# Edge sums of a graph kernel: from TensorE products in step 0 to VectorE and ScalarE in step 1

## The chip, the core and the metric

The kernel runs on one core of a Trainium2 chip. Its engines are TensorE (PE in the profile, with PEld for its weight loads), VectorE (DVE), ScalarE (ACT), GpSimd (POOL) and SyncE (SP); each takes its instructions from its own queue. The metric is the device time of one execution in microseconds (us), less is better.

## What is computed

Four graph layers over 4096 nodes with 256 features each, all with the same 0/1 adjacency of 4096 x 4096, each layer with a residual and a layer norm. Layer 1 is the long one: two steps, and in each a row-normalised neighbour product (`R @ Xf`) and a top-p attention (`A @ Xa`).

```python
# layer 0
agg = adj @ x / jnp.maximum(deg, 1.0)
relu(concat([x, agg]) @ W + b)
# layer 1, for n in range(2)
A = _top_p_attention(Xa, W1, W2, W3)
Xf = R @ Xf
Xa = A @ Xa
Z = Z + Xf @ U1[n].T + Xa @ U2[n].T
# layer 2, called with edge_features = adj
neighbor_node_features = adj @ node_features
neighbor_edge_features = jnp.einsum('ij,ji->i', adj, edge_features)[:, None]
support = concat((node_features, neighbor_node_features, neighbor_edge_features))
return support @ weight + bias
# layer 3
out = A_norm @ x
relu(out @ W + b)
```

The change concerns `neighbor_edge_features`: for each node i the sum over j of `adj[i, j] * adj[j, i]`. Both factors are 0 or 1, so it is the number of edges that exist in both directions. The kernel holds it in `nef`, one column for each tile of 128 nodes, and layer 2 alone reads it.

## The kernel before

The 4096 nodes are 32 tiles (NT) of 128 rows. Layer 0 reads the adjacency as float32, turns it into bytes (u8) on the way, and stores the bytes in device memory as `adj8_d`, one block for each tile. Layers 2 and 3 stream the adjacency again.

Layer 1 is built by `run_step(n, es)`, once for each step n. Its loop goes over i from -2 to 31. In one turn three tiles are at work: tile i is weighted with its attention and multiplied out (`st`), tile i + 1 has its threshold found (`cd`), and the logits of tile i + 2 are made (`nxt`). `pieces` writes this turn out in 8 chunks (NLC) of 512 nodes. A chunk holds the logits of `nxt` (`logits_chunk`, copied from PSUM to `e` by ACT at L381), the attention product of `st`, a chunk of a neighbour product (`neighbours`) and small operations given in `ops`. In step 0 attention is sparse: 16 rows gathered by POOL (`gather`, L638) and multiplied by diagonal matrices (L729). In step 1 it is dense: transposes (L712), a copy to `at` by ACT (L715), and matmuls (L737). DVE looks for the largest logits (MAX8, L399, L494), takes single values out (MATCH_REPLACE8, L624) and masks what falls below the threshold (L629). ACT makes the exponentials, in step 1 of a whole row of 4096 in one instruction (L422). Rows whose threshold needs more search are put off and done by a second pass (`put_off`, names ending in `_l`).

`neighbours(n, i, g, acc_r, pn, xf)` is the neighbour product of tile i, chunk g: SP loads 8 blocks of bytes for two chunks (`adj8`, three buffers), ACT widens them to `adjq` (L649), PE multiplies four blocks of 128 x 512 into `acc_r` (L652). Where `pn` is given, which is in step 0 only, it also makes the edge sums: POOL loads blocks of the other orientation as bytes (`adjn8`, L658), ACT widens them (L661), and PE multiplies the same four `adjq` blocks by them into `pn` (L664). After all 32 blocks the diagonal of `pn` is what is wanted; DVE multiplies by the identity and sums (L678) in `r_end`. `pn` lies in the PSUM buffer tagged `nef`. Because of that, step 0's `acc_r` has the one buffer `acc`, and `r_acc` lets tiles alternate between `acc` and `nef` only after `nef_done`.

Neighbour products need no attention, so they run ahead where PE is free: four tiles before the first attention tile of step 0, the first five of step 1 at the end of step 0, six more at the start of step 1 (`FIRST`), and one in a turn after that.

After a tile, `after` mixes both results (`mix`, L790 and L792), and in step 1 takes two layer norms, in each of which DVE makes the variance, POOL the power -1/2 (`rstd`, L192) and DVE the rest (L816, L197). POOL also writes the list of rows that are put off (L572). SP loads what `fetch` asks for (L773) and stores results (L761, L680).

The program is not executed in the order of the text: a scheduler places the instructions of each engine into one fixed order when the program is built, by priority and by its own idea of when operands are there. Waits between engines are semaphores. A buffer of a pool (`bufs=2`) is given out again when its last reader is done, and the instruction that writes it next waits for that in its engine's queue.

Of the kernel before, what the change touches and what calls it, by code (L numbers as in the profile page):

```python
# [21 lines left out]
P = 128  # L22
# [23 lines left out]


@with_exitstack
def gnn_stack(ctx, tc, x, adjt, adjn, w0, b0, w1, w2t, w3t, u1t, u2t, ln_g, ln_b, w2, b2, w3, b3, out):

# [267 lines left out]

    with tc.tile_pool(name="l1", bufs=1, reuse_waits="tile") as l1:

        cur = {"late": False, "n": 0, "nef_done": False}


        FIRST = [[range(k * NT // 16, (k + 1) * NT // 16) for k in range(2)]]
# [61 lines left out]
        def small(tag, w=1, dt=F32, bufs=2):  # L388
            if cur["late"]:
                return cur["lw"].tile([P, w], dt, tag=tag, name=f"{tag}_l", bufs=2 if w == 1 else 1)  # L390
            return work.tile([P, w], dt, tag=tag, name=tag, bufs=bufs)
# [248 lines left out]

        GP = LC // P

        def neighbours(n, i, g, acc_r, pn, xf):

            if g % 2 == 0:
                cur["a8"] = cur["w"].tile([P, 2 * GP, P], U8, tag="adj8", name="adj8", bufs=3)
                nc.sync.dma_start(cur["a8"], adj8_d[i][:, g * GP : (g + 2) * GP, :])
            a = cur["w"].tile([P, GP, P], F32R, tag="adjq", name="adjq", bufs=2)
            nc.scalar.copy(a, cur["a8"][:, g % 2 * GP : (g % 2 + 1) * GP, :])  # L649
            for j in range(GP):  # L650
                jt = g * GP + j
                nc.tensor.matmul(acc_r, a[:, j, :], xf[:, jt, :], start=(jt == 0), stop=False)  # L652
            if g + 1 == NLC:
                nc.tensor.matmul(acc_r, ident_r, xf[:, i, :], start=False, stop=True)
            if pn is not None:
                if g % (NLC // 2) == 0:
                    cur["b8"] = cur["w"].tile([P, NT // 2, P], U8, tag="adjn8", name="adjn8", bufs=2)
                    nc.gpsimd.dma_start(cur["b8"], adjn[i, :, g * GP : g * GP + NT // 2, :])  # L658
                b = cur["w"].tile([P, GP, P], F32R, tag="adjn", name="adjn", bufs=2)
                k = g % (NLC // 2) * GP  # L660
                nc.scalar.copy(b, cur["b8"][:, k : k + GP, :])  # L661
                for j in range(GP):
                    jt = g * GP + j
                    nc.tensor.matmul(pn[:, :P], a[:, j, :], b[:, j, :], start=(jt == 0),  # L664
                                     stop=(jt == NT - 1))

        def r_acc(i):

            return ps_acc.tile([P, 512], F32, tag=("acc", "nef")[i % 2 if cur["nef_done"] else 0], name="acc_r", bufs=1)

        def r_end(i, acc_r, pn):
            xf_new = work.tile([P, D], F32, tag="xf_new", name="xf_new", bufs=1)
            nc.scalar.activation(xf_new, acc_r[:, :D], AF.Copy, scale=rs[:, i : i + 1])
            nc.vector.scalar_tensor_tensor(xf_new, acc_r[:, D:], rs[:, i : i + 1], xf_new, op0=ALU.mult, op1=ALU.add)
            if pn is not None:

                junk = spare_row.bitcast(F32)[:, :P]
                nc.vector.scalar_tensor_tensor(junk, pn[:, :P], 1.0, ident, op0=ALU.mult, op1=ALU.mult,  # L678
                                               accum_out=nef[:, i : i + 1])
            nc.sync.dma_start(rows(xf_d, i), xf_new)  # L680

        def r_product(n, i, xf):

            acc_r, pn = r_acc(i), None
            if n == 0:
                pn = ps_acc.tile([P, 512], F32, tag="nef", name="nef_ps", bufs=1)
            for g in range(NLC):
                neighbours(n, i, g, acc_r, pn, xf)
            r_end(i, acc_r, pn)

        def pieces(n, st, nxt, ops, rs_now=()):


            G = GP
            few = st is not None and sparse(st)
            if st is not None:
                e = st["e"]
                acc_a = half("acc")
                if "xf" not in st:
                    fetch(n, st)  # L700
            with_r = st is not None and len(rs_now) > 0
            if with_r:
                i, = rs_now
                acc_r, pn = r_acc(i), None
                if n == 0:
                    pn = ps_acc.tile([P, 512], F32, tag="nef", name="nef_ps", bufs=1)
            ats = {}

            def turn(g):
                ps = ps_tr.tile([P, 4, P], F32, tag="tr", name="at_ps")  # L710
                for j in range(G):
                    nc.tensor.transpose(ps[:, j, :], e[:, (g * G + j) * P : (g * G + j + 1) * P], ident)  # L712
                at = cur["w"].tile([P, G, P], F32, tag="at", name="at", bufs=2)
                ats[g] = at
                nc.scalar.copy(at[:, :G, :], ps[:, :G, :])  # L715

            if st is not None and not few:
                turn(0)
            for g in range(NLC):
                if nxt is not None:  # L720
                    logits_chunk(nxt["e"], nxt["q"], g)
                if few:
                    per = KEPT // NLC
                    for k in range(g * per, (g + 1) * per):
                        if k % 4 == 0:
                            dg = cur["w"].tile([P, 4, P], F32, tag="at", name="dg", bufs=2)
                            nc.vector.tensor_mul(dg, ident[:, None, :].to_broadcast([P, 4, P]),
                                                 st["w"][:, k : k + 4, None].to_broadcast([P, 4, P]))
                        nc.tensor.matmul(acc_a, dg[:, k % 4, :], st["G"][k], start=(k == 0), stop=(k == KEPT - 1))  # L729
                        if k + 8 < KEPT:  # L730
                            gather(st, k + 8)
                elif st is not None:
                    if g + 1 < NLC:
                        turn(g + 1)
                    for j in range(G):
                        jt = g * G + j
                        nc.tensor.matmul(acc_a, ats[g][:, j, :], cur["xa"][:, jt, :], start=(jt == 0),  # L737
                                         stop=(jt == NT - 1))
                if with_r:
                    neighbours(n, i, g, acc_r, pn, cur["xf"])  # L740
                for f in ops.get(g, ()):
                    f()
            if st is None:
                for i in rs_now:
                    r_product(n, i, cur["xf"])
            else:
                xa_new = work.tile([P, D], F32, tag="xa_new", name="xa_new", bufs=1)
                nc.scalar.activation(xa_new, acc_a, AF.Copy, scale=st["sc"])
                if n + 1 < STEPS:
                    put(xa_d, st, xa_new)  # L750
                st["xa"] = xa_new
            if with_r:
                r_end(i, acc_r, pn)

        def put(dst, st, t):

# [27 lines left out]
        def mix(n, st):  # L784

            xt = transposed(st["xf"], st["xa"])
            ps = half("mm")
            for c in range(4):
                u = cur["u1" if c < 2 else "u2"]
                nc.tensor.matmul(ps, xt[:, c, :], u[:, c % 2, :], start=(c == 0), stop=(c == 3))  # L790
            h = work.tile([P, D], F32, tag="h", name="h")
            nc.vector.tensor_add(h, ps, st["res"])  # L792
            if n + 1 < STEPS:
                put(h_d, st, h)

                ps = half("mm")
                for c in range(2):
                    nc.tensor.matmul(ps[:, :P], xt[:, 2 + c, :], w3t_sb[:, c, :], start=(c == 0), stop=(c == 1))
                up = upper(ps[:, :P])
                kt = work.tile([P, P], F32, tag="kt", name="kt", bufs=1)  # L800
                nc.scalar.copy(kt[:, :DA], up[:, :DA])
                nc.vector.tensor_sub(kt[:, DA:], ps[:, DA:P], up[:, DA:])
                put(k_d, st, kt)
            return h
# [78 lines left out]
        def run_step(n, es):  # L883
# [93 lines left out]
            if n == 0:  # L977
                for fs in last:
                    for f in fs:
                        f()  # L980
                last = []
                cur["late"] = True
                fetch(n, jobs[0]["st"])
                cur["late"] = False
                cur["nef_done"] = True
                for i in range(FIRST[1][0][0]):
                    r_product(1, i, cur["next"])
            for job in jobs:
                last = finish(job, last)
            for fs in last:  # L990
# [141 lines left out]
```

## Time and profile before

The median of three runs is 3377.89 us (3377.06 to 3378.86). The profile is of one more execution, which was somewhat longer.

| | us |
|---|---|
| median of the runs | 3377.89 |
| the profiled execution's own time | 3410.96 |
| its span, first to last instruction | 3409.3 |
| PE busy in it | 3032.2 (89%) |
| DVE busy | 2382.9 (70%) |
| ACT busy | 1598.1 (47%) |
| POOL busy | 920.8 (27%) |
| first and last edge product (L664) | 396.7 and 1308.7 |

From the times at which lines start, layer 0 takes the span to about 341 us, step 0 of layer 1 to about 1455, step 1 to about 2790, layers 2 and 3 the rest. Shares over the whole span mix these stages, which have different limits, so they are to be read stage by stage. A busy engine is counted from the start of an instruction to its end; PE's matmuls overlap, so a sum of their durations is more than they take. "Idle before, releaser" in a line of the profile is the time that the engine stood still just before instructions of that group, and what ended it.

### The profile page before, as it was taken

How to read it: one execution, taken by the hardware profiler on the slowest of the kernel's cores; microseconds unless marked ns; L12 is line 12 of the kernel's file. 1: busy time of each engine (PE TensorE's matmuls, PEld its weight loads, DVE VectorE, ACT ScalarE, POOL GpSimd, SP SyncE). 2: the span in 40 equal slices, each digit the busy share in tenths (PEclk: the TensorE clock that was granted, in tenths of full speed). 3: DMA queues.
4: the chain of work that ended last, by engine and by line, in shares of the span. 5: the costliest groups of instructions: out<-in, count | busy, mean ns of one | idle time of the engine just before them, and what ended most of it. 6: DMA issues, size and time to landing. Idle time of an engine off the chain costs nothing. (4 is left out here: it accounts for less than half of the span.)

```text
span 3409.3 us, 46023 instructions
## 1 busy us (share of the span) xinstructions
PE 3032.2 (89%) x14780; PEld 2486.4 (73%) x14780; DVE 2382.9 (70%) x7082; ACT 1598.1 (47%) x2846; POOL 920.8 (27%) x1170
## 2 busy tenths in 40 slices
PE   5999879999999997789989899989997549999998
PEld 4888667777777775568877677877786437887776
DVE  6888858777777776357988886989799654443333
ACT  4555656666766764455555454645553211111000
POOL 1111246666666664100000001001000112222332
PEclk9999999999999997889999999999999769999999
DMA  8888357777777775141001110011011038888887
GB/s 156 149 141 136 73 98 117 130 135 132 133 131 132 132 133 132 61 131 30 24 22 23 33 38 26 30 32 38 29 38 19 15 103 247 244 247 244 266 270 227
DMA packets 233760, 383.52 MB, mean 112 GB/s; under 512 B 33089, under 2 KB 158849, under 8 KB 233505
## 3 DMA queue, kind: packets, MB, share of 16 engines
q0 software_dynamic: 83328, 238.78, 35.3%
q1 hardware_dynamic: 133200, 125.72, 13.1%
q10 hardware_dynamic: 16976, 15.95, 1.5%
q8 instruction: 120, 1.97, 0.3%
q14 instruction: 136, 1.11, 0.1%
HBM read 423.45 MB, written 57.54 MB: 141 GB/s over the span
## 5 line engine op out<-in xcount | busy, mean ns | idle before, releaser
L652 PE MATMUL acc_r<-xh,adjq 128*128 128x512 f32 x2048 | 615.8, 431 | 31.3 <-ACT adjq L649 21.0
L737 PE MATMUL acc_bank<-xa,at 128*128 128x256 f32 x2304 | 568.2, 388 | 31.0 <-ACT at L715 30.4
L638 POOL DMA_INDIRECT G<-x_d,cols x512 | 498.8, 974 | 331.4 <-PE acc_bank L729 159.7
L737 PEld LDWEIGHTS acc_bank<-xa,at 128*128 128x128 f32 x2304 | 425.5, 194 | 92.7 <-ACT at L715 41.3
L652 PEld LDWEIGHTS acc_r<-xh,adjq 128*128 128x128 f32 x2048 | 379.9, 192 | 131.7 <-ACT adjq L649 46.5
L399 DVE MAX8 cand<-e 128x8 f32<-128x256 f32 x1024 | 381.8, 415 | 130.0 <-ACT e L381 115.8
L649 ACT CAST adjq<-adj 128x512 fp32r<-128x512 uint8 x512 | 316.0, 619 | 312.9 <-issue 94.2
L380 PE MATMUL lg<-kS,q 128*128 128x512 f32 x1104 | 395.6, 444 | 17.8 <-ACT e L381 10.2
L381 ACT COPY e<-lg 128x512 f32<-128x512 f32 x552 | 320.2, 586 | 193.7 <-PE lg L380 171.0
L192 POOL TENSOR_TENSOR rstd<-ve,mhalf 128x1 f32<-128x1 f32 x168 | 103.3, 615 | 899.9 <-DVE ve L190 853.3
L729 PE MATMUL acc_bank<-G,dg 128*128 128x256 f32 x1024 | 275.1, 390 | 33.7 <-DMA G<-x_d,cols 26.7
L496 DVE FIND_INDEX8 cols<-top,e 128x8 uint32<-128x4096 f32 x64 | 282.8, 4419 | 0.0
L168 PE MATMUL acc<-xh,adjt 128*128 128x512 f32 x1024 | 261.5, 407 | 22.7 <-ACT xh L144 18.0
L168 PE MATMUL acc<-yh,adjt 128*128 128x512 f32 x1024 | 257.4, 403 | 3.8 <-DMA adjt<-in_adjt 3.4
L168 PE MATMUL acc<-xh,a 128*128 128x512 f32 x1024 | 258.1, 404 | 1.6 <-ACT a L251 1.6
L729 PEld LDWEIGHTS acc_bank<-G,dg 128*128 128x128 f32 x1024 | 193.9, 193 | 82.7 <-DMA G<-x_d,cols 36.0
L137 POOL DMA_DIRECT2D adjt<-in_adjt x256 | 139.6, 545 | 419.8 <-PE acc L168 316.9
L715 ACT COPY at<-at_ps 128x512 f32<-128x512 f32 x296 | 173.9, 589 | 148.3 <-PE at_ps L712 146.9
L168 PEld LDWEIGHTS acc<-xh,adjt 128*128 128x128 f32 x1024 | 192.3, 191 | 67.9 <-ACT xh L144 19.1
L168 PEld LDWEIGHTS acc<-yh,adjt 128*128 128x128 f32 x1024 | 189.8, 188 | 49.0 <-DMA adjt<-in_adjt 4.1
L168 PEld LDWEIGHTS acc<-xh,a 128*128 128x128 f32 x1024 | 191.4, 189 | 43.9 <-ACT a L251 1.7
L712 PE MATMUL at_ps<-ident,e 128*128 128x128 f32 x1184 | 183.6, 279 | 42.9 <-DVE e L629 29.1
(277 smaller groups left out, 4948.4 us busy)
## 6 DMA issues: line engine op xcount, KB each, us to landing
adjt<-in_adjt POOLq DMA_DIRECT2D x256, 512.0 KB
adj<-adj_d SPq DMA_DIRECT2D x256, 128.0 KB
a<-in_adjt POOLq DMA_DIRECT2D x64, 256.0 KB
adj_d<-a SPq DMA_DIRECT2D x64, 256.0 KB
adjn<-in_adjn POOLq DMA_DIRECT2D x64, 256.0 KB
x_d<-x SPq DMA_DIRECT2D x64, 128.0 KB
G<-x_d,cols POOLq DMA_INDIRECT x512
xf_d<-xf_new SPq DMA_DIRECT2D x64, 128.0 KB
```

What stands on the lines that cost most here:

```text
L168: nc.tensor.matmul(acc, a[:, j, :], halves(jt), start=(jt == 0), stop=(jt == NT - 1))
L380: nc.tensor.matmul(pl[:, :LC], q[k], kS[:, s], start=(k == 0), stop=(k == 1))
L381: nc.scalar.copy(l[:, s], pl[:, :LC])
L399: nc.vector.max(dst[:, 8 * g : 8 * g + 8], src[:, g * GW : (g + 1) * GW])
L496: nc.vector.max_index(st["at"][:, 8 * r : 8 * r + 8], t8, st["e"][:, :N])
L638: nc.gpsimd.indirect_dma_start(out=g, out_offset=None, in_=x1_d, in_offset=bass.IndirectOffsetOnAxis(ap=st["at"][:, k : k + 1], axis=0))
L649: nc.scalar.copy(a, cur["a8"][:, g % 2 * GP : (g % 2 + 1) * GP, :])
L652: nc.tensor.matmul(acc_r, a[:, j, :], xf[:, jt, :], start=(jt == 0), stop=False)
L712: nc.tensor.transpose(ps[:, j, :], e[:, (g * G + j) * P : (g * G + j + 1) * P], ident)
L715: nc.scalar.copy(at[:, :G, :], ps[:, :G, :])
L729: nc.tensor.matmul(acc_a, dg[:, k % 4, :], st["G"][k], start=(k == 0), stop=(k == KEPT - 1))
L737: nc.tensor.matmul(acc_a, ats[g][:, j, :], cur["xa"][:, jt, :], start=(jt == 0), stop=(jt == NT - 1))
```

## The change

The edge products leave step 0. In step 1, for each of the 32 tiles and each of 8 chunks, POOL loads 128 x 512 bytes of the adjacency's rows (`r8`) and as many of its transpose's rows (`c8`), both cast from float32 on the way and in two buffers each. DVE takes the bitwise AND of the two, read as 128 x 128 int32. ACT copies the result over `c8`, which nobody reads, and sums it along the row into one of 8 columns of `ns`. After the last chunk DVE adds the 8 columns into `nef`. Three things go along: `adj8` is loaded chunk by chunk, 64 KB in place of 128 KB, still with three buffers; `acc_r` alternates between `acc` and `nef` in both steps; `kt` comes from the step's own pool. The inputs are the adjacency and its transpose (`adjr`, `adjc`) in place of the blocked `adjn`.

```diff
-        def neighbours(n, i, g, acc_r, pn, xf):
-
-            if g % 2 == 0:
-                cur["a8"] = cur["w"].tile([P, 2 * GP, P], U8, tag="adj8", name="adj8", bufs=3)
-                nc.sync.dma_start(cur["a8"], adj8_d[i][:, g * GP : (g + 2) * GP, :])
+        def neighbours(i, g, acc_r, xf):
+
+            a8 = cur["w"].tile([P, GP, P], U8, tag="adj8", name="adj8", bufs=3)
+            nc.sync.dma_start(a8, adj8_d[i][:, g * GP : (g + 1) * GP, :])
             a = cur["w"].tile([P, GP, P], F32R, tag="adjq", name="adjq", bufs=2)
-            nc.scalar.copy(a, cur["a8"][:, g % 2 * GP : (g % 2 + 1) * GP, :])
+            nc.scalar.copy(a, a8)
...
-            if pn is not None:
-                if g % (NLC // 2) == 0:
-                    cur["b8"] = cur["w"].tile([P, NT // 2, P], U8, tag="adjn8", name="adjn8", bufs=2)
-                    nc.gpsimd.dma_start(cur["b8"], adjn[i, :, g * GP : g * GP + NT // 2, :])
-                b = cur["w"].tile([P, GP, P], F32R, tag="adjn", name="adjn", bufs=2)
-                k = g % (NLC // 2) * GP
-                nc.scalar.copy(b, cur["b8"][:, k : k + GP, :])
-                for j in range(GP):
-                    jt = g * GP + j
-                    nc.tensor.matmul(pn[:, :P], a[:, j, :], b[:, j, :], start=(jt == 0),
-                                     stop=(jt == NT - 1))
-
         def r_acc(i):
-
-            return ps_acc.tile([P, 512], F32, tag=("acc", "nef")[i % 2 if cur["nef_done"] else 0], name="acc_r", bufs=1)
...
+            return ps_acc.tile([P, 512], F32, tag=("acc", "nef")[i % 2], name="acc_r", bufs=1)
+
+        def edge_sums(i, g):
+
+            if g == 0:
+                cur["ns"] = small("ns", NLC)
+            s = slice(g * LC, (g + 1) * LC)
+            r8, c8 = (cur["w"].tile([P, LC], U8, tag=k, name=k, bufs=2) for k in ("r8", "c8"))
+            nc.gpsimd.dma_start(r8, rows(adjr, i)[:, s])
+            nc.gpsimd.dma_start(c8, rows(adjc, i)[:, s])
+            r32 = r8.bitcast(I32)
+            nc.vector.tensor_tensor(r32, r32, c8.bitcast(I32), op=ALU.bitwise_and)
+            nc.scalar.activation(c8, r8, AF.Copy, accum_out=cur["ns"][:, g : g + 1])
+            if g + 1 == NLC:
+                nc.vector.tensor_reduce(nef[:, i : i + 1], cur["ns"], axis=AX.X, op=ALU.add)
...
-            if pn is not None:
-
-                junk = spare_row.bitcast(F32)[:, :P]
-                nc.vector.scalar_tensor_tensor(junk, pn[:, :P], 1.0, ident, op0=ALU.mult, op1=ALU.mult,
-                                               accum_out=nef[:, i : i + 1])
...
+                if n > 0 and st is not None and st["tile"] is not None:
+                    edge_sums(st["tile"], g)
                 if with_r:
-                    neighbours(n, i, g, acc_r, pn, cur["xf"])
+                    neighbours(i, g, acc_r, cur["xf"])
...
-                kt = work.tile([P, P], F32, tag="kt", name="kt", bufs=1)
+                kt = cur["w"].tile([P, P], F32, tag="kt", name="kt", bufs=1)
```

More of the change, by code (lines that the diff above doesn't have):

```diff
@@ L48, in gnn_stack @@
 @with_exitstack
-def gnn_stack(ctx, tc, x, adjt, adjn, w0, b0, w1, w2t, w3t, u1t, u2t, ln_g, ln_b, w2, b2, w3, b3, out):
+def gnn_stack(ctx, tc, x, adjt, adjr, adjc, w0, b0, w1, w2t, w3t, u1t, u2t, ln_g, ln_b, w2, b2, w3, b3, out):
     nc = tc.nc
@@ L321, in gnn_stack @@
     with tc.tile_pool(name="l1", bufs=1, reuse_waits="tile") as l1:
-        cur = {"late": False, "n": 0, "nef_done": False}
+        cur = {"late": False, "n": 0}
         FIRST = [[range(k * NT // 16, (k + 1) * NT // 16) for k in range(2)]]
@@ L654, in neighbours, with r_end @@
                 nc.tensor.matmul(acc_r, ident_r, xf[:, i, :], start=False, stop=True)
-            if pn is not None:
-                if g % (NLC // 2) == 0:
-                    cur["b8"] = cur["w"].tile([P, NT // 2, P], U8, tag="adjn8", name="adjn8", bufs=2)
-                    nc.gpsimd.dma_start(cur["b8"], adjn[i, :, g * GP : g * GP + NT // 2, :])
-                b = cur["w"].tile([P, GP, P], F32R, tag="adjn", name="adjn", bufs=2)
-                k = g % (NLC // 2) * GP
-                nc.scalar.copy(b, cur["b8"][:, k : k + GP, :])
-                for j in range(GP):
-                    jt = g * GP + j
-                    nc.tensor.matmul(pn[:, :P], a[:, j, :], b[:, j, :], start=(jt == 0),
-                                     stop=(jt == NT - 1))
-        def r_acc(i):
-            return ps_acc.tile([P, 512], F32, tag=("acc", "nef")[i % 2 if cur["nef_done"] else 0], name="acc_r", bufs=1)
-        def r_end(i, acc_r, pn):
+        def r_acc(i):
+            return ps_acc.tile([P, 512], F32, tag=("acc", "nef")[i % 2], name="acc_r", bufs=1)
[11 more added lines that the diff above has]
+                nc.vector.tensor_reduce(nef[:, i : i + 1], cur["ns"], axis=AX.X, op=ALU.add)
+        def r_end(i, acc_r):
             xf_new = work.tile([P, D], F32, tag="xf_new", name="xf_new", bufs=1)
@@ L674, in r_end, with r_product @@
             nc.vector.scalar_tensor_tensor(xf_new, acc_r[:, D:], rs[:, i : i + 1], xf_new, op0=ALU.mult, op1=ALU.add)
-            if pn is not None:
-                junk = spare_row.bitcast(F32)[:, :P]
-                nc.vector.scalar_tensor_tensor(junk, pn[:, :P], 1.0, ident, op0=ALU.mult, op1=ALU.mult,
-                                               accum_out=nef[:, i : i + 1])
             nc.sync.dma_start(rows(xf_d, i), xf_new)
[L682 to L686, printed above, removed]
+        def r_product(i, xf):
+            acc_r = r_acc(i)
             for g in range(NLC):
-                neighbours(n, i, g, acc_r, pn, xf)
-            r_end(i, acc_r, pn)
+                neighbours(i, g, acc_r, xf)
+            r_end(i, acc_r)
         def pieces(n, st, nxt, ops, rs_now=()):
@@ L703, in pieces @@
                 i, = rs_now
-                acc_r, pn = r_acc(i), None
-                if n == 0:
-                    pn = ps_acc.tile([P, 512], F32, tag="nef", name="nef_ps", bufs=1)
+                acc_r = r_acc(i)
             ats = {}
@@ L744, in pieces @@
                 for i in rs_now:
-                    r_product(n, i, cur["xf"])
+                    r_product(i, cur["xf"])
             else:
@@ L752, in pieces @@
             if with_r:
-                r_end(i, acc_r, pn)
+                r_end(i, acc_r)
         def put(dst, st, t):
@@ L984, in run_step @@
                 cur["late"] = False
-                cur["nef_done"] = True
                 for i in range(FIRST[1][0][0]):
-                    r_product(1, i, cur["next"])
+                    r_product(i, cur["next"])
             for job in jobs:
@@ L1105 @@
         "adjt": blocks.transpose(0, 3, 2, 1),
-        "adjn": blocks.transpose(2, 1, 0, 3),
+        "adjr": adj,
+        "adjc": adj.T,
         "w0": L0_gnn_W,
```

## The prediction

> **What bounds the kernel now.** I read the busy time by stage, then what TensorE (PE) waits for in each stage, then single tiles in order of time. Step 0 of the attention layer is 340 to about 1455 us, step 1 from there to about 2790. The first view is busy time per window (window, length, then busy us and count of PE, weight loads, DVE, ACT, POOL, then clock and DMA share). The first two lines are the steady part of step 0 and step 1; the next two one tile of step 1 without a neighbour product and one with.
>
> ```profile
> 540.00:1280.00 740.00, 686.52 (x3604) 578.98 (x3603) 569.12 (x1662) 509.22 (x1011) 457.99 (x493) 1.00 0.75 132
> 1455.00:2567.00 1112.00, 1025.29 (x5114) 841.17 (x5115) 925.87 (x3071) 589.91 (x990) 85.71 (x104) 0.97 0.15 38
> 1594.00:1622.30 28.30, 27.03 (x144) 22.69 (x143) 25.69 (x91) 15.02 (x25) 2.24 (x3) 1.00 0.08 24
> 2465.30:2499.30 34.00, 32.84 (x168) 27.26 (x167) 33.05 (x113) 18.37 (x33) 2.23 (x3) 1.00 0.12 35
> ```
>
> Step 0 is PE's: 93% busy, DVE 77%, ACT 69%. Step 1 belongs to two engines: PE 92% and DVE 83% over the stage, but in the tile at 2465 PE is busy for 32.84 and DVE for 33.05 of 34.00 us. ACT is at half, POOL nearly idle. So the change takes work from the one bound engine of step 0 and puts some on an engine that is full in parts of step 1.
>
> PE in order of time, in step 0, shows what an edge product holds it up:
>
> ```profile
> 1012.46 1.28 PE L652 MATMUL acc_r<-xh,adjq 128*128 128x512 f32 x4
> 1013.58 0.56 PE L664 MATMUL nef_ps<-adjn,adjq 128*128 128x128 f32 x4
> 1013.97 0.67 PE L380 MATMUL lg<-kS,q 128*128 128x512 f32 x2
> ...
> 1018.30 1.27 PE L652 MATMUL acc_r<-xh,adjq 128*128 128x512 f32 x4
> 1019.41 0.56 PE L664 MATMUL nef_ps<-adjn,adjq 128*128 128x128 f32 x4
> 1019.80 0.41 PE L178 MATMUL tr<-ident,x 128*128 128x128 f32 x2
> ```
>
> The next work starts 0.39 us after four edge products start (1013.58 to 1013.97, 1019.41 to 1019.80). The 0.56 beside them overlaps what follows, so I price by starts.
>
> Groups by line and shape, step 0 first (DVE's tensor_tensor, POOL's gathers), then step 1:
>
> ```profile
> L727 DVE TENSOR_TENSOR dg<-ident,w 128x512 f32<-128x512 f32 x104 | 71.0, 682 | 10.9 <-PE acc_bank L729 8.3 <-issue 2.1
> L638 POOL DMA_INDIRECT G<-x_d,cols x416 | 402.1, 967 | 253.7 <-PE acc_bank L729 114.5 <-issue 76.2 <-PE nef_ps L664 26.5
> L649 ACT CAST adjq<-adj 128x512 fp32r<-128x512 uint8 x171 | 105.7, 622 | 134.5 <-PE acc_r L652 68.8 <-issue 31.2 <-DMA adj<-adj_d 29.7
> L624 DVE MATCH_REPLACE8 e<-match,e 128x4120 f32<-128x4120 f32 x28 | 124.2, 4435 | 0.3 <-issue 0.3
> L422 ACT ACTIVATE e<-e,m 128x4096 f32<-128x4096 f32 x28 | 104.1, 3718 | 18.3 <-DVE m L432 18.3
> L364 DVE TENSOR_TENSOR q<-mm_bank,upk 128x128 fp32r<-128x128 f32 x32 | 8.9, 279 | 0.0
> L192 POOL TENSOR_TENSOR rstd<-ve,mhalf 128x1 f32<-128x1 f32 x60 | 38.2, 636 | 660.7 <-DVE ve L190 625.0 <-DVE pb_l L457 10.0 <-DVE cs L515 9.7
> ```
>
> Two blocks matter: MATCH_REPLACE8 holds DVE for 4.4 us and the exp holds ACT for 3.7 us, each once a tile. Whatever stands behind them waits.
>
> [...]
>
> **The change part by part.**
>
> *Removed from PE in step 0.* Each of 32 tiles has 8 groups of four edge products: 8 x 0.39 = 3.1 us a tile, 101 us in all. A steady tile of step 0 takes about 28.4 us (740 over 26) with PE busy 26.4. Without the products PE has 23.3. Next in line: DVE 569/26 = 21.9 less the 0.36 us diagonal read (0.28 and its accumulator's 0.08) = 21.5; POOL 16 gathers at 0.97 plus the 0.30 us that stands before each back-to-back one, and the list write, 1.3: 21.6. All fit below PE, but with 1.8 us less cover each, so I keep 0.2 us of the gain back: 28 steady tiles x 2.9 = 81. The four neighbour products ahead of the first attention tile give 4 x 3.1 less idle PE there, about 8. *Removed from ACT and POOL in step 0:* 256 casts of 0.62 (159 us), and 64 issues of 0.6 us. In the first tiles POOL waited 41 us, in its order, for cast buffers, with gathers behind it; I count 3 us. Step 0: -92, between -65 (DVE or POOL take over with stalls) and -110 (all of it and the start).
>
> *Added to DVE in step 1.* 256 ANDs over 128 int32 at 0.28 and 32 reduces at 0.13 (as L632's): 76 us, 2.4 us a tile. [...] In the tile without a neighbour product DVE goes from 25.7 to 28.1 of 28.3: I take +1.1 us. In the tight tile from 33.05 to 35.4 of 34.0: with its 0.95 us idle kept, +2.3. Some tiles leave DVE 5 us or more idle: +1.5. With 8, 12 and 12 tiles of these kinds: 9 + 28 + 18 = 55. Bounds for this item: 0 (all in idle time: DVE has 186 us of it in the 1112) and +76.
>
> *Added to ACT in step 1.* 256 sums at 0.61 plus an accumulator read of 0.19 (as behind L418): 205 us, 6.4 a tile, 18.4 to 24.8 of 34. Room enough on average, but the order of the built program puts them between the copies at (L715) and e (L381) that feed PE, often two right around the exp. PE lost 30 us to at and 12 to adjq in step 1 already. Bounds 0 to +50; I take +5.
>
> *Added to POOL in step 1.* 512 issues at 0.6 + 0.3: 460 us on an engine with 86 us of work. Behind each stand rstd (L192) and the list write; DVE waited 22 us for rstd. An issue waits for a free buffer, which a sum on ACT releases. Bounds 0 to +60; I take 0, since the other work that DVE has in its order hides one issue.
>
> *Moved on SP.* adj8 loads become 512 of 64 KB, 0.32 us each to issue, and three buffers hold 3 chunks in place of 6. In step 1 ACT already waited 29.7 us in nine waits for these loads. In a 34 us tile three chunks are 12 us ahead, and the xf load (L773) held SP for up to 23 us. Bounds 0 to +25; taken within the 5 of ACT.
>
> *One answer:* acc and nef alternating from the start (PE waited 0.6 us for xf_new, once), kt in another pool: 0.
>
> Sum: -92 + 55 + 5 = -32 us on the profiled execution of 3410.96 (span 3409.3 and 1.7 around it), 3379. The median of the runs is 0.9903 of the profiled one, which gives 3346.
>
> **The rivals.**
>
> *B, the ANDs find DVE's idle time.* For it: the scheduler sets many between the pairs of MAX8 that wait for e, where DVE had 21 us of waits. Against: in tight tiles there is nearly none. Step 1 +20, net -72, median 3307.
>
> *C, the round trip of two buffers paces step 1: slower.* A chunk's r8/c8 pair is used in turn by POOL (two issues, 1.8), DMA[...], DVE (0.28) and ACT (0.8). [...] Each trip may also wait behind MATCH_REPLACE8 (4.4) or the exp (3.7), and queues that take turns hold everything behind: ACT's at copy behind a sum whose AND is late, DVE behind a landing, rstd behind an issue. [...] +4 us a tile, 32 x 4 = 128; net +36, median about 3413. Against: in the built order the MATCH_REPLACE8 and the four masks behind it mostly stand between two ANDs, so that landings and sums can pass under them.
>
> *D, step 0 gives little back.* DVE's 21.5 and POOL's 21.6 of work are in fixed order with PE; if a tile stops at 26.8, step 0 gives 50; with step 1 at +50, median 3378.
>
> That the products do not go is excluded: the built program has no matmul into nef_ps.
>
> **How the numbers follow.** The sum above 0.48, B 0.15, C 0.27, D 0.10. The first case's own range is 3313 to 3370; its bad end gives 0.01 to slower and 0.01 to no change. D is no change 0.08, else split; C gives 0.01 to no change. Faster by over 0.2% (6.8 us, about what this kernel's measurement can tell) 0.62, within 0.10, slower 0.28. The range takes in B and most of C: 3300 to 3420.
>
> **What would show it.** Step 0: a steady tile of 25.5 us; over 26.5 is D. Step 1: stage 60 us longer, DVE over 90% busy; if it is over 100 us longer with DVE below 88% and DVE, ACT or POOL waiting on r8, c8 or each other at the AND, it is C. rstd waits well over 22 us would mean that POOL's queue cost something that I set at 0. Waits for adj above 60 us would mean the same of SP. I am wrong if layers 2 and 3 move at all, or if the AND takes much other than 0.28 us.

## The result, and the profile after

The changed kernel takes 3419.03 us (median of 4 runs, 3417.12 to 3426.66), the kernel before 3377.47 us beside it. The ratio is 1.0129 (95% interval 1.0111 to 1.0147): some 42 us slower, where the prediction had 32 us faster as the likeliest case. The time is within the range and close to the 3413 of rival C.

The profiled execution of the changed kernel (3420.0 us, span 3418.2) lies at its median; the one of the kernel before lay 33 us above its own. So the two profiles are compared for where time is spent, and sums of time are taken from ratios of runs.

Busy time by window of the changed kernel: window, length, busy us and count of PE, weight loads, DVE, ACT, POOL, then clock, DMA share and GB/s.

```profile
540.00:1200.00 660.00, 610.06 (x2844) 498.18 (x2843) 580.28 (x1693) 415.06 (x817) 456.43 (x468) 0.97 0.64 140
1455.00:2567.00 1112.00, 945.57 (x4517) 775.19 (x4516) 870.61 (x2980) 635.96 (x1266) 308.06 (x514) 0.93 0.48 51
```

Step 0 gained: its steady tile, measured between the starts of ACT's scaled copies into `xa_new`, went from 28.6 us in the profile before to 23.6, and its last tile ends at 1198 in place of 1373. Step 1 lost it again: its steady tile went from 34.0 to 39.3. In the second line the engines of step 1 are *less* busy than before, although DVE and ACT have more to do: PE has 85% where it had 92%, DVE 78% where it had 83%. So step 1 isn't longer because an engine is full. DMA's share rose from 0.15 to 0.48, and PE's granted clock fell from 0.97 to 0.93. Layers 2 and 3 did not move: from the last layer norm of layer 1 to the end it is 626 us before and 627 after.

What the engines wait for in step 1 (1403 to 2600 us): engine and waiting instruction, releaser, us in total, times, longest.

```profile
POOL r L663 <- ACT c L667: 531.7, 133, 20.8
ACT c L667 <- DVE r L666: 190.6, 96, 8.5
DVE r L666 <- DMA c<-in_adjc: 154.3, 82, 8.9
...
PE mm_bank L558 <- DVE bad L530: 40.3, 16, 3.9
...
PE acc_bank L728 <- ACT at L706: 32.9, 16, 8.5
...
ACT adjq L648 <- DMA adj<-adj_d: 24.4, 12, 4.9
...
DVE h L197 <- POOL rstd L192: 10.0, 23, 1.3
DVE h L809 <- POOL rstd L192: 8.5, 23, 0.9
```

The AND is L666, the sum L667, the loads L663 and L664. The three engines wait in a ring: POOL for a buffer that ACT's sum frees, ACT for the AND, DVE for the load. What stands behind a waiting instruction in POOL's order waits with it: in the next view `c` is issued at 1551.56, 0.52 us behind an `r` that waited 6.13 us. The two `rstd` lines (18.5 us) show that POOL's other work was hardly missed; but the loads themselves start as late as the wait ends. DVE's 154 us are new: in step 1 of the kernel before, all of DVE's waits for transfers made 22.4 us. PE's wait for `bad`, which DVE makes, grew from 15 us to 40.

The same in order of time. A fence of the timeline has start, duration, engine, line, operation, and in brackets the idle time before it and what ended that.

```profile
1551.04 0.53 POOL L663 DMA_DIRECT2D r<-in_adjr  x1 [6.13 <-ACT c L667]
...
1551.56 0.54 POOL L664 DMA_DIRECT2D c<-in_adjc  x1
...
1555.40 0.29 DVE L666 TENSOR_TENSOR r<-r,c 128x128 int32<-128x128 int32 x1 [0.83 <-DMA c<-in_adjc]
1555.61 0.42 DVE L785 TENSOR_TENSOR h<-mm_bank,res 128x256 f32<-128x256 f32 x1
1555.78 0.63 ACT L667 ACTIVATE c<-r 128x512 uint8<-128x512 uint8 x1 [1.75 <-DVE r L666]
...
1556.08 0.71 PE L360 MATMUL mm_bank<-xt,wq_sb 128*128 128x128 f32 x4 [0.66 <-DVE h L785]
```

`c` is issued at 1551.56 and usable at 1555.40, 3.84 us later. `h` has nothing to do with the edges, but stands behind the AND in DVE's order, and PE's next product waits for `h`. Here each loses under a microsecond; over step 1, the starts of the 256 loads and ANDs show that 103 of the ANDs come after more than 0.15 us of idle DVE. For these late ones the median from the issue of `c` to the AND is 4.26 us.

Before these 103 ANDs DVE stood 197 us in all. Some of the waits are much longer than a microsecond. One of them:

```profile
1532.59 1.82 POOL L572 DMA_INDIRECT list_d<-ids,slots  x1 [4.00 <-DVE slots L566]
...
1534.41 0.56 POOL L663 DMA_DIRECT2D r<-in_adjr  x1
...
1534.97 0.53 POOL L664 DMA_DIRECT2D c<-in_adjc  x1
...
1542.52 0.29 DVE L666 TENSOR_TENSOR r<-r,c 128x128 int32<-128x128 int32 x1 [5.12 <-DMA c<-in_adjc]
1542.85 0.63 ACT L667 ACTIVATE c<-r 128x512 uint8<-128x512 uint8 x1 [4.76 <-DVE r L666]
...
1544.58 1.12 PE L703 MATMUL at_ps<-ident,e 128*128 128x128 f32 x4 [5.29 <-ACT at L706]
```

The AND at 1542.52 is that of the loads issued at 1534.41 and 1534.97. Just ahead of them POOL issued the list of put-off rows (L572). The load is usable only 7.55 us after its issue, and DVE, ACT and PE stand still one behind the other for some five microseconds each. Of the 13 pairs of loads whose first was issued within 4 us of the start of a list write, nine made DVE wait, 44 of the 197 us: six of them for 5.1 to 8.9 us, three for about a microsecond. That the write holds the loads up is read from these starts and was not tried.

How often the ring itself is in the way can be read from the same starts. For 62 of the 103 late ANDs, POOL could issue the first load only when ACT's sum had freed the buffer, so that the whole trip of a buffer lay in front of them. They hold 100 of the 197 us.

### The profile page after: what moved, and what is told of

It is laid out like the page before. It is cut to its first block, busy times and chain, and to the rows that moved or that the text cites. A ratio compares the mean times of both kernels' runs of the same rounds, so it can differ in the third digit from the quotient of the medians.

```text
span 3418.2 us, 46103 instructions
## 1 busy us (share of the span) xinstructions
PE 2956.8 (87%) x13756; PEld 2405.0 (70%) x13756; DVE 2414.1 (71%) x7306; ACT 1625.3 (48%) x3102; POOL 1163.6 (34%) x1618
## 3 DMA queue, kind: packets, MB, share of 16 engines
q0 software_dynamic: 147840, 255.58, 44.7%
q1 hardware_dynamic: 170064, 125.74, 12.6%
HBM read 490.56 MB, written 57.54 MB: 160 GB/s over the span
## 5 line engine op out<-in xcount | busy, mean ns | idle before, releaser
L651 PE MATMUL acc_r<-xh,adjq 128*128 128x512 f32 x2048 | 639.6, 438 | 46.7 <-ACT adjq L648 42.9
L728 PE MATMUL acc_bank<-xa,at 128*128 128x256 f32 x2304 | 593.5, 400 | 40.0 <-ACT at L706 39.4
L728 PEld LDWEIGHTS acc_bank<-xa,at 128*128 128x128 f32 x2304 | 440.0, 201 | 111.3 <-ACT at L706 54.5
L651 PEld LDWEIGHTS acc_r<-xh,adjq 128*128 128x128 f32 x2048 | 392.0, 196 | 145.1 <-ACT adjq L648 66.1
L663 POOL DMA_DIRECT2D r<-in_adjr x256 | 139.6, 545 | 754.1 <-ACT c L667 657.2
L667 ACT ACTIVATE c<-r 128x512 uint8<-128x512 uint8 x256 | 161.1, 630 | 260.9 <-DVE r L666 235.1
L720 PEld LDWEIGHTS acc_bank<-G,dg 128*128 128x128 f32 x1024 | 192.6, 195 | 99.2 <-issue 23.4
L380 PEld LDWEIGHTS lg<-kS,q 128*128 128x128 f32 x1104 | 200.9, 197 | 70.6 <-ACT e L381 40.1
```

The source lines that it names most:

```text
L380: nc.tensor.matmul(pl[:, :LC], q[k], kS[:, s], start=(k == 0), stop=(k == 1))
L667: nc.scalar.activation(c8, r8, AF.Copy, accum_out=cur["ns"][:, g : g + 1])
```

## The experiments

The kernel before ran at 3357 to 3419 us in the four groups of runs, so all kernels are compared by their ratio to the kernel before in the same group. The changed kernel's is 1.0129; 0.01 is 34 us. Theory 1 in the expectations is rival C in its several forms: what is lost is lost in waiting for the loads. The other numbers are its rivals, and each expectation says what they hold; that the added instructions themselves cost it, that the count or traffic of loads does, or the load of `adj8`.

### One part of the change at a time

**The adj8 part alone.** The kernel before, with `adj8` loaded in single chunks.

```diff
-            if g % 2 == 0:
-                cur["a8"] = cur["w"].tile([P, 2 * GP, P], U8, tag="adj8", name="adj8", bufs=3)
-                nc.sync.dma_start(cur["a8"], adj8_d[i][:, g * GP : (g + 2) * GP, :])
+            cur["a8"] = cur["w"].tile([P, GP, P], U8, tag="adj8", name="adj8", bufs=3)
+            nc.sync.dma_start(cur["a8"], adj8_d[i][:, g * GP : (g + 1) * GP, :])
```

> The kernel before with adj8 loaded chunk by chunk, three buffers of 64 KB: this part of the change alone. Theory 3: 30 us or more slower than before. Theories 1 and 2: within 10 us of before.

1.0004 (0.9995 to 1.0013). SP's queue is not the cause.

**The removal alone.** The changed kernel without its edge sums.

```diff
+    nc.vector.memset(nef, 0.0)
...
-                    edge_sums(st["tile"], g)
+                    pass
```

> The edge sums are left out of step 1 altogether (nef is set to zero), the rest as in the changed kernel. This prices the removal by itself, with adj8 in single chunks. All theories: step 0 as in the changed kernel. Theories 1 and 2: step 1 back to about 1320 us, so the time is 175 to 200 below the changed kernel, near 3230. Theory 3: step 1 keeps 50 us or more of its growth, near 3280 or above.

0.9668 (0.9652 to 0.9684): the removal, with the small parts that go along, is worth 112 us, more than the forecast. What is added in step 1 costs the difference to the changed kernel, 0.0461 or 156 us, where the forecast had 60.

**The added instructions without their loads.**

```diff
-            nc.gpsimd.dma_start(r8, rows(adjr, i)[:, s])
-            nc.gpsimd.dma_start(c8, rows(adjc, i)[:, s])
...
-            nc.vector.tensor_tensor(r32, r32, c8.bitcast(I32), op=ALU.bitwise_and)
+            nc.vector.tensor_tensor(r32, w3t_sb[:, 0, :].bitcast(I32), w3t_sb[:, 1, :].bitcast(I32), op=ALU.bitwise_and)
```

> Leaves out both loads: every AND reads two blocks of the same size that lie in SBUF all through step 1, and ScalarE sums its result as before, so the count of edges is that of other data. Nothing waits for a transfer. Theory 1: the instructions cost what the prediction gave them, 60 us over the 3267 without sums, so 3310 to 3340 us. Rival 4: most of the 152 us stays, 3380 us or more. Rival 5: within 20 us of 3267.

0.9595 (0.9572 to 0.9618), which is 25 us *faster* than without any sums. Theory 1 had too much cost; rival 5, for which only loads cost, is the nearest. Both builds have their own order of instructions, and the 25 us are not explained; but 256 ANDs, 256 sums and 32 reduces by themselves don't make step 1 longer. Rival 4 falls.

**The loads without the instructions.**

```diff
-            nc.vector.tensor_tensor(r32, r32, c8.bitcast(I32), op=ALU.bitwise_and)
-            nc.scalar.activation(c8, r8, AF.Copy, accum_out=cur["ns"][:, g : g + 1])
...
+                nc.vector.memset(cur["ns"], 0.0)
```

> Leaves out the bitwise ANDs and the sums of ScalarE: both loads of every chunk stay, with the same two pairs of buffers, and nothing reads them; the count of edges is zero. Theory 1 (VectorE, in its fixed order, stands at an AND until the load has landed): the loads alone cost next to nothing, 3265 to 3290 us, near the 3267 of the kernel without any sums. Rival 4 (the added instructions of VectorE and ScalarE themselves crowd the stage): the same here. Rival 5 (the 512 loads cost by themselves, through GpSimd's queue or the DMA engines): 3340 us or more.

1.045 (1.0433 to 1.0468). By the number this is rival 5, but the trace shows another program: with no reader to pace them, all loads were placed between 1286 and 1907 us, and POOL stood in them, with `rstd` behind. POOL's loads of `r` in its timeline (other lines left out), and then a line of the waits over the whole run:

```profile
1527.11 0.53 POOL L664 DMA_DIRECT2D r<-in_adjr  x1
...
1529.61 0.53 POOL L664 DMA_DIRECT2D r<-in_adjr  x1
...
1532.16 0.53 POOL L664 DMA_DIRECT2D r<-in_adjr  x1 [0.27 <-DMA r<-in_adjr]
```

```profile
DVE h L808 <- POOL rstd L192: 213.0, 32, 62.4
```

So the run doesn't tell the theories apart. It gives one number: with two pairs of buffers and nobody reading, a pair of loads takes 2.5 us (1527.11 to 1529.61 to 1532.16).

**The sum on ACT alone left out.**

```diff
+                nc.vector.memset(cur["ns"], 0.0)
...
-            nc.scalar.activation(c8, r8, AF.Copy, accum_out=cur["ns"][:, g : g + 1])
```

> Loads and ANDs stay, the sum on ACT is left out (nef becomes zero), so that the AND frees both buffers. Theory 1: the trip loses ACT's 0.8 us and the wait of ACT for a late AND (190 us), so DVE's waits for c8 fall to under a half and 120 to 170 us of the growth go; 3250 to 3300. Theory 2: 205 us of ACT work go, but ACT was not full, so 20 to 50 us; 3370 to 3400.

1.0263 (1.0233 to 1.0293), a miss of both theories: with less work it is slower than the whole change. DVE's wait for the loads stayed (163 us against 154), though each pair is free at once after the AND. The build has another order, and why it costs more is open. For the same reason it doesn't show what a buffer freed earlier would be worth in the order of the changed kernel.

### Buffers and the place of the AND

Each of these builds has its own order of instructions. The resident kernel moved by 25 us without a known cause, so a difference of that size between two of them is not secured.

**A third pair**, in memory that step 1 doesn't use.

```diff
+            if g % 3 == 2:
+                r8, c8 = (w3t_sb[:, k, :].bitcast(U8) for k in range(2))
+            else:
+                r8, c8 = (cur["w"].tile([P, LC], U8, tag=k, name=k, bufs=2) for k in ("r8", "c8"))
```

> A third r8/c8 pair for chunks 2 and 5 of each tile, in memory that step 1 does not use; the same loads, ANDs and sums. Theory 1 (the round trip of two buffer pairs holds DVE, then ACT, then PE): a quarter to a half of the 154 us that DVE waits for c8 goes, and the time falls by 40 to 90 us against the changed kernel, to 3330 to 3380. Theory 2 (the added DVE and ACT work itself lengthens step 1): no more than 15 us. Theory 3 (adj8 in single chunks): nothing.

1.0053 (1.0036 to 1.007): 26 us better than the change, less than theory 1 asked for and more than theory 2 did. DVE's wait in step 1 falls from 154 to 114 us.

**One pair.** `bufs=2` becomes `bufs=1`.

> The whole change with one pair of buffers in place of two, so that a load can be issued only when the sum before it has ended. Theory 1: each AND then waits a whole trip of issue and landing, the wait of VectorE for loads grows from 154 to 300 us or more, and the time to 3480 to 3700 us. Rival 4: within 20 us of the 3419 of the whole change. Rival 5: also within 20 us, since the number of loads is the same.

1.097 (1.0947 to 1.0994), 3699 us, as theory 1 expected. The waits over the whole run:

```profile
POOL r L663 <- ACT c L667: 1012.0, 198, 27.4
...
ACT c L667 <- DVE r L666: 553.8, 178, 10.9
DVE r L666 <- DMA c<-in_adjc: 502.1, 187, 10.4
```

Now 187 of the 256 ANDs wait. The number of pairs matters: from one to two it is worth 284 us, from two to three 26. With two pairs most of the trip is hidden, but not all: whether an AND comes late depends on how far DVE's fixed order sets it behind the AND two chunks earlier, which used the same buffers. A trip, from an AND to the landing of the next load into its buffers, takes some 6.1 us in the changed kernel (a sum of medians: 0.33 from the AND to ACT's sum where ACT waits, 1.02 to the next issue, 0.52 to the second issue, 4.26 to a late AND). Leaving out the wait itself, the starts of the two ANDs lie less than that apart 72 times, and 62 of these are late; of the other 182, 40 are.

**One load for both halves.** The inputs are laid side by side, so that 256 loads of twice the size take the place of 512.

```diff
-            r8, c8 = (cur["w"].tile([P, LC], U8, tag=k, name=k, bufs=2) for k in ("r8", "c8"))
-            nc.gpsimd.dma_start(r8, rows(adjr, i)[:, s])
-            nc.gpsimd.dma_start(c8, rows(adjc, i)[:, s])
+            rc = cur["w"].tile([P, 2, LC], U8, tag="rc8", name="rc8", bufs=2)
+            nc.gpsimd.dma_start(rc, adjrc[i * P : (i + 1) * P, g, :, :])
+            r8, c8 = rc[:, 0, :], rc[:, 1, :]
```

> The whole change with the adjacency and its transpose laid side by side in memory, so that one load brings both halves of a chunk: 256 loads of twice the size in place of 512, two buffers of 1 KB. Theory 1: the second half need no longer wait 0.5 us for GpSimd to issue it, and only one landing is waited for: 10 to 40 us less than 3419, VectorE's wait for loads 100 to 140 us. Rival 5: half the issues cost half, 3350 us or less. Rival 4: within 10 us of 3419.

1.0218 (1.0195 to 1.0242), slower by 30 us, and DVE's wait rose to 175 us in step 1: all three theories missed. Half the issues brought nothing, and with one pair of buffers the same number of loads cost 284 us more. That speaks against rival 5 in the form that the count of loads costs; the bytes are the same in all three kernels.

**The AND one chunk later than its loads.**

```diff
-                    edge_sums(st["tile"], g)
+                    late_rc = cur.get("rc")
+                    edge_sums(st["tile"], g)
+                    if g > 0:
+                        edge_sum(st["tile"], g - 1, late_rc)
```

`edge_sums` only loads here; `edge_sum` has the AND and the sum. The last chunk's follows at the end of the tile.

> The whole change, with the AND and the sum of a chunk written one chunk after its loads, so that the scheduler places them later against their loads; same buffers, same transfers. Theory 1b (VectorE's fixed order reaches the ANDs before the loads have landed, and a later place cures it): VectorE's wait for the loads at most 80 us, time 3300 to 3370 us. Rival 7 (with two pairs a later AND also frees the pair later, so the next load starts later and the wait stays): wait 120 us or more, 3400 us or more.

1.0159 (1.0136 to 1.0181), DVE's wait 147 us: rival 7, no gain.

**Both, the lag and the third pair.**

> As the kernel with the AND one chunk later, and a third pair of buffers for every third chunk in memory that step 1 doesn't use. Theory 1: a pair more and a chunk more of distance together take most of the wait, at most 50 us of it stay, 3290 to 3350 us, which would beat both kernels. Rival 7: the third pair brings as little as alone (23 us) over the kernel with two pairs and the lag.

1.0004 (0.9991 to 1.0017): no difference from the kernel before. DVE's waits at the ANDs in step 1, over all three pairs, are 99 us in place of 154. That takes back all of the loss, but not more: theory 1 had the direction and too much of it. The third pair brings twice what it brought without the lag, 52 us in place of 26, which speaks against rival 7.

### The transfer's length

**The same bytes from a u8 source.** Both loads read the copy that layer 0 stored as bytes.

```diff
-            nc.gpsimd.dma_start(r8, rows(adjr, i)[:, s])
-            nc.gpsimd.dma_start(c8, rows(adjc, i)[:, s])
+            for t in (r8, c8):
+                nc.gpsimd.dma_start(t.rearrange("p (j m) -> p j m", m=P), adj8_d[i][:, g * GP : (g + 1) * GP, :])
```

> Both loads of a chunk read the same count of bytes from the copy of the adjacency that device memory already holds as u8 (64 KB read in place of 256 KB of float32, no cast on the way), so the AND sees other data. All five engines have the same instructions in the same order as in the whole change; only the transfer is shorter. Theory 1a (the landing's length, set by the float32 transfer, is what VectorE stands for): VectorE's wait for these loads falls from 154 to 30 to 90 us in step 1 and the time to 3300 to 3370 us. Rival 6 (the trip's fixed parts, the issue and the landing of any load, and the order of the queues): wait 120 us or more and 3395 us or more.

0.9767 (0.9745 to 0.9789). Against the changed kernel this is 0.0362 or 122 us, with every engine's instructions in the same order: the one comparison here that no new order blurs. The gain is at the far end of what theory 1a expected or beyond it, and rival 6 falls. Windows, waits in step 1, the list of transfers (KB each as they land, median us from issue to landing) and a piece of the timeline:

```profile
1455.00:2567.00 1112.00, 982.89 (x4874) 810.03 (x4872) 946.89 (x3217) 677.33 (x1351) 343.41 (x563) 0.96 0.21 55
```

```profile
ACT c L667 <- DVE r L666: 130.9, 82, 7.7
...
DVE r L666 <- DMA c<-adj_d: 75.3, 31, 9.6
```

```profile
r<-adj_d POOLq DMA_DIRECT2D x256, 64.0 KB, 2.2
c<-adj_d POOLq DMA_DIRECT2D x256, 64.0 KB, 2.4
```

```profile
1545.30 0.53 POOL L664 DMA_DIRECT2D r<-adj_d  x1 [5.79 <-ACT c L667]
...
1545.82 0.53 POOL L664 DMA_DIRECT2D c<-adj_d  x1
...
1548.59 0.27 DVE L666 TENSOR_TENSOR r<-r,c 128x128 int32<-128x128 int32 x1
```

Issue of `c` to AND is 2.77 us here, and DVE doesn't wait. Over step 1 its wait is halved, 31 times in place of 82. DVE is back at 85%, PE at 88% with a clock of 0.96. The queue that carries POOL's transfers says what went. Its line gives packets, MB as they land, and the time that the packets took as a share of the 16 DMA engines' span, for the changed kernel and then here (the line of q1 keeps its 170064 packets, 12.6% and 12.9%):

```profile
q0 software_dynamic: 147840, 255.58, 44.7%
```

```profile
q0 software_dynamic: 90496, 255.58, 34.6%
```

44.7% of 3418.2 us less 34.6% of 3275.3 us is 395 us, or 1.5 us for each of the 256 pairs. The medians from the issue of `c` to a late AND differ by about as much, 4.26 and 2.79 us. The loads land as 64 KB in both, but the profiles have 490.56 MB read from HBM for the changed kernel and 389.89 here: 100.67 MB less, or 192 KB for each of the 512 loads, the difference of 256 KB of float32 to 64 KB of bytes.

The u8 source takes away the conversion too. Single packets in the trace of the changed kernel point to the bytes: one of a casting load (2 KB read, 512 bytes landed) takes 98 ns in the median, one of 512 bytes without a cast (the loads of `adj8`) 27 ns, one of 2 KB without a cast (the stores of `adj8_d` in layer 0) 84 ns. A load of float32 without the cast was not tried.

**Half of it in the whole computation.** The transpose's half of a chunk can be read from the stored bytes, in pieces of 128 bytes; added to the kernel with the lag and the third pair.

```diff
-    adj8_d = [dram.tile([P, NT, P], U8, name=f"adj8_{it}_d") for it in range(NT)]
+    adj8_all = dram.tile([NT, P, NT, P], U8, name="adj8_all_d")
+    adj8_d = [adj8_all[it] for it in range(NT)]
...
-            nc.gpsimd.dma_start(c8, rows(adjc, i)[:, s])
+            nc.gpsimd.dma_start(c8.rearrange("p (k m) -> p k m", m=P),
+                                adj8_all[g * GP : (g + 1) * GP, :, i, :].rearrange("k p m -> p k m"))
```

> The whole computation. As the kernel with the AND one chunk later and a third pair of buffers, and the transpose's half of every chunk loaded from the bytes that layer 0 stored (four pieces of 128 bytes per partition; the 32 stored blocks lie in one tensor for that), so that only the other half is a float32 transfer. Every engine's order is that of the kernel with the lag and the third pair. Theory 1a (what is lost hangs on the float32 transfers' length): VectorE's wait for these loads falls from 76 us in step 1 to 50 or less, and 25 to 60 us go, 3300 to 3335 us, faster than both kernels. Rival 8 (the small pieces take the DMA engines as long as the float32 rows did): within 12 us of 3359.

1.0153 (1.0127 to 1.0179), slower than the same without the bytes (1.0004); both sides missed. The stage that the edit aims at hardly moved (DVE's waits at the ANDs 95 us after 99, a step-1 tile 36.7 us after 36.9), although the DMA share in the window of step 1 fell from 0.50 to 0.40; why the waits stayed is open. The loss is in step 0, which has none of these loads. A stretch of step 0, here and then in the kernel with the lag and the third pair:

```profile
600.00:800.00 200.00, 166.97 (x727) 133.23 (x728) 148.19 (x432) 108.82 (x214) 114.94 (x119) 0.93 0.48 111
```

```profile
600.00:800.00 200.00, 190.94 (x903) 157.49 (x902) 184.25 (x545) 134.28 (x264) 142.95 (x146) 0.99 0.64 137
```

A tile of step 0 takes 27.9 us against 23.4, with the same instructions in the same order. The blocks lie in one tensor in place of 32, and it ran on a chip on which the kernel before was slower as well (3419 us). Which of these did it was not tried apart. No version faster than the kernel before that does the whole work was found.

## Why the prediction was wrong

*The direction.* The sum had -92 + 55 + 5. The runs give -112 for what was removed and +156 for what was added. By ratios, the 156 split into three: -25 for ANDs and sums on resident data (0.9595 against 0.9668), +58 when their operands are loaded as bytes (0.9767 against 0.9595), +122 because they are loaded as float32 (1.0129 against 0.9767). Only the last term is between builds of one order; the first two carry the unexplained shifts of a new order.

*Step 0, -92.* Right in mechanism, too small. The steady tile is 23.6 us, not 25.5. Against the 27.4 of the kernel with only adj8 changed, whose time is that of before, each of 8 groups of edge products gave 0.47 us, not the 0.39 less a cover kept back (with `acc` and `nef` alternating, which no run takes apart). DVE (88% of the window) and POOL (69%) did not take over, and rival D falls. The excess of the profiled execution of before lay in this stage too (28.6 us a tile against 27.4).

*Added to DVE, +55, with POOL at 0: the step that failed.* The durations were right: in step 1 the AND took 0.287 us, forecast 0.28. The sum priced the ANDs as busy time and asked where DVE had room; in the resident kernel they cost nothing. The wait for their loads it put at 0, "since the other work that DVE has in its order hides one issue". That work did not hide it: DVE stood still before 103 of the 256 ANDs, 197 us in all, 185 of them by the profile for the landing of `c`, and what stands behind the AND in DVE's order stood with it (`h` above, 0.83 us). A cost for this was found only under rival C.

*Rival C, 0.27.* It named the ring of POOL, DMA, DVE and ACT, and had 3413; a step-1 tile grew by 4.7 us (34.6 with adj8 alone to 39.3) where it had 4. Its signs came as written: step 1 far longer, DVE below 88%, three engines waiting at the AND. It got too little weight for two reasons. How long such a load takes to land was the author's estimate, not shown by a run or trace of the kernel before, and it was too short for the loads that DVE waited for: with the float32 source the AND came 4.26 us after the issue of `c`, and the trip took 6.1 us; the u8 source gave 2.2 and 2.4, and 2.79 where DVE waited. And the argument against it held only in part. Where an instruction of over 1 us (MATCH_REPLACE8 or a mask for the most part) stood on DVE between two ANDs that used the same buffers, 38 of 153 were late; where none did, 64 of 101.

That 3413 came so close is luck in part. The 112 and 156 us stand there as 92 and 128. And the 128, 4 us in every one of the 32 tiles, was the author's estimate, which rested on the landing that was not shown. (A smaller slip: 32 times 8 times 0.39 is 100, not 101.)

*ACT, +5.* Not shown by itself. A sum took 0.630 us and its read of the accumulator 0.191, forecast 0.61 and 0.19. ACT's own sums cost nothing on resident data; it waited for late ANDs, 190.6 us at L667, but 80.6 us of such waits stand in the resident kernel too; and PE's wait for `at` rose only from 30 to 33 us.

*POOL, 0.* Right about `rstd`: 18.5 us of waits, forecast to stay near 22. What was missed is the other direction: not work behind the loads, but, as the starts have it, loads behind the list write.

*SP.* Right: 1.0004 alone, and 24.4 us of waits for `adj` in place of 29.7, and 43.2 over the whole of step 1, below the 60 that it named. *Layers 2 and 3* did not move, as forecast.

What stays open: what the fall of PE's clock adds (0.93 against 0.96 with u8 sources, one order; the neighbour product L651 takes 451 against 437 ns in step 1). It comes with the waits, and no run has one without the other. From the first tile of step 1 to the 26th, PE is busy for 877.5 us with float32 sources and 842.2 with u8, while the stretch itself falls from 1043.7 to 941.0; so at most some 35 of these 103 us can be slower matmuls, an estimate from these four times.

## What to carry to other kernels

Don't price a load with a cast on the way by the bytes that land: here both sources landed 64 KB a load, but float32 had 256 KB read for it, and float32 with its cast in place of bytes was 122 of 156 us. An instruction that needs a fresh load can hold up its engine's whole order until the landing, and the busy share doesn't show it: DVE stood 197 us before the late ANDs, and its share in step 1 went from 83% to 78%. So work out the trip from issue to free buffer and compare it with the distance at which the built order sets load and use. When a step's own prices are sure and its waits are not, the waits decide the weight of the rival.

## What the runs showed of the hardware

- The u8 loads of 64 KB landed 2.2 and 2.4 us after their issue (medians of the 31 and 33 landings that the trace has). With 256 KB of float32 as the source of each, it was 3.15 us at the least and 4.26 in the median from the issue of the second of two casting loads to a late AND. Two such loads one behind the other with no reader took 2.5 us a pair in the stretch shown; with 512 KB read for a pair that is some 210 GB/s, an estimate from these two numbers.
- Where POOL issued a pair of loads within 4 us of the start of the list write (L572, 128 single values), a late AND came 9.2 us after the issue of the second (median of nine), against 4.2 for the other late ones. With u8 sources it was 7.0 (seven) and 2.6. That the write is the cause was not tried.
- With instructions and order unchanged, PE's clock in step 1 went from 0.93 to 0.96 when the waits for the loads were halved.
